# A selective-scan kernel: the convolved map is read piece by piece from DRAM, the decays move from PSUM to SBUF, and their banks become second buffers

## The chip, the cores and the metric

The kernel runs on one core of a Trainium2 chip. A core has five engines that run their own instruction streams and wait for each other by semaphores: PE (TensorE, matrix products), DVE (VectorE), ACT (ScalarE), POOL (GpSimd) and SP (SyncE, which here issues the transfers). SBUF is the working memory of 128 partitions; PSUM is the small memory of eight banks that PE writes its sums to. The metric is the device time in microseconds. The kernel before took 12172.9 us (median of three runs, 12171.95 to 12176.84).

## The reference, cut to what matters

Two layers of a state-space block run one after the other on 8 images of 64x64 positions and 96 channels. The first layer is the costly one. It projects 96 channels to 192, applies a 3x3 convolution per channel and a SiLU, which gives the map `xc`, and scans that map in four directions with 16 states per channel:

```python
xs = _cross_scan(xc)      # rows, columns, and both reversed
delta = softplus(dt_projs_w @ (x_proj_w @ xs)[:R] + bias)
def step(h, inp):
    u_t, d_t, B_t, C_t = inp
    dA = jnp.exp(d_t[..., None] * A)
    h = dA * h + d_t[..., None] * B_e * u_t[..., None]
    return (h, jnp.sum(h * C_e, axis=-1))
...
y = ys + u * D            # the skip term
y = _cross_merge(y)       # sum of the four directions
y = layernorm(y) * silu(z) @ out_proj_w.T
```

The second layer has a scan of the same kind whose sums matter only near the ends of the map, and the kernel computes only those (the "short" sets below).

## The kernel before

Positions lie along the free axis. The 192 channels are two halves (`h`) of 96 partitions. For the scan 32 channels x 4 states fill the 128 partitions, so one half is three groups (`g`) of 32 channels, and one group needs four sets (`i`) of four states. A set on 1024 positions is one recurrence on a 128x1024 tile. Per image there are four directions (`k`) x four pieces of 1024 positions ("units") x 2 halves x 3 groups x 4 sets = 384 sets, 3072 in all.

`scan_rows` writes the order of work out by hand: a loop over sets n, in which each engine gets what belongs to the sets around n. For a set, in this order:

- `fetch` (five sets ahead) has SP load `dt_rep` and `dtu_rep` (delta and delta*u of 32 channels, each copied to four partitions), once per group; `replicate` (four ahead) loads `b_rep` and `c_rep`.
- `fill` (one ahead, L940): ACT makes `decay` = exp(A x delta). The tile lies in PSUM, in the pool `pslot` of two buffers of two banks.
- `drive` (two ahead, L957): ACT copies delta*u of the group to PSUM, `pdrive`, one buffer of two banks.
- `advance_set` (L974 and L987): for three sets of four DVE multiplies `drive` by `b_rep` into `set`; for all four DVE then runs the scan in place, `set` = `decay` x previous + `set`. For the fourth set `early` has POOL make the product (L964), from SBUF's `dtu_rep`.
- `keep_state` (L998): ACT keeps the last column for the next piece.
- `read_out` (one behind, L1003): POOL multiplies `set` by `c_rep` into `out`.
- `collect` (three behind, L1030 and L1039): PE adds the old value of the sum (for the first direction the map times the skip weight `skip0`, for the others `y`) and gathers the states of each channel into `acc`, one PSUM bank; `release` (L1069) has ACT copy `acc` to `y`.

There are four `set` buffers and four `out` buffers. Between these, a plan of steps puts work of other stages into the same loop: `projection` and `ready_by_time` prepare a unit two units ahead (their PSUM bank is `pmisc`, one buffer), with POOL's delta*u (`take_product`, L606) and two stores by SP; `conv_beside` makes the second layer's map of the image before and the first layer's map of the image after, 512 positions at a time, with the bank of `pmisc`, and stores it to DRAM.

The map of an image, 32 KB per partition, lies whole in SBUF, in the pool `keep` of two buffers, the other being `y`. `next_map` loads the next image's map over the old one in four pieces near the end of the scan. PSUM is full: decays four banks, drive two, `acc` one, `pmisc` one.

The short sets of the second layer (48 in all, 960 columns) use the same buffers, with one more DVE multiplication (L977) by `cum_rep`.

Between two scans `between` runs the output phase (normalization, gate, output projection) of the image and prepares the first deltas of the next (`first_deltas`, `ready_first`, L658 to L660); `begin` does the first convolution and the first deltas; `finish` ends the last image.

Of the kernel before, what the change touches and what calls it, by code (L numbers as in the profile page):

```python
# [52 lines left out]
def two_ss2d_layers(ctx: ExitStack, tc: tile.TileContext, t: dict, out: bass.AP):  # L53
# [16 lines left out]
    keep = ctx.enter_context(tc.tile_pool(name="keep", bufs=2))  # L70
# [47 lines left out]
    w["skip0"] = const.tile([C, NH, C], F32, name="skip0")  # L118
    for h in range(NH):
        nc.vector.tensor_scalar(  # L120
            w["skip0"][:, h, :], w["eye"], w["dsum0"][:, h : h + 1], None, ALU.mult
        )

# [264 lines left out]

    def like(ap, by_column):

        return ap.rearrange("p (a b) -> p a b", b=HH) if by_column else ap
# [39 lines left out]
    def scan_rows(xc, y, parts, plan, rows, beside):  # L431

        with (
            tc.tile_pool(name="loads", bufs=2, side="right") as loads,
            tc.tile_pool(name="piece", bufs=1) as piece,
            tc.tile_pool(name="work", bufs=2) as work,
            tc.tile_pool(name="pslot", bufs=2, space=PSUM) as pslot,
            tc.tile_pool(name="pdrive", bufs=1, space=PSUM) as pdrive,
            tc.tile_pool(name="pacc", bufs=1, space=PSUM) as pacc,
            tc.tile_pool(name="pmisc", bufs=1, space=PSUM) as pmisc,
        ):  # L450
            units, jobs, sets, x_dbl = parts
            total = len(sets)
            plan = plan(pmisc)
            with tc.manual_schedule():
                state = None
                arena = piece.tile([P, 4 * T], F32, name="arena")
                plan.setdefault(-1, []).insert(0, lambda: low_rows(x_dbl, units[1], rows))
                for n in range(-AHEAD, max(total + 4, max(plan, default=0) + 1)):
                    at = lambda i: sets[n + i] if 0 <= n + i < total else None
                    m, j = divmod(n + 1, PER)  # L460
                    if j == 0 and 0 <= m < len(jobs):

                        stages = []
                        if m + 2 < len(jobs):
                            prepare = short_ready if jobs[m + 2]["unit"]["short"] else ready_by_time
                            stages += prepare(xc, x_dbl, jobs[m + 2], arena, pmisc)
                        if m % NH == 1 and m // NH + 2 < len(units):
                            unit = units[m // NH + 2]
                            project = short_projection if unit["short"] else projection
                            stages += project(xc, x_dbl, unit, rows, pmisc)  # L470
                        for step, stage in stages:
                            plan.setdefault(n + step, []).append(stage)
                    fetch(at(AHEAD), False, loads)
                    fetch(at(2), True, loads)
                    replicate(at(AHEAD_BC), x_dbl, loads)
                    replicate_short(at(AHEAD_BC), "b", loads)
                    replicate_short(at(AHEAD_BC - 1), "c", loads)
                    if at(0) and at(0)["unit"]["nth"] == 0 and at(0)["first"]:
                        state = piece.tile([P, D // GC * NS], F32, name="state0", bufs=2)
                    advance_set(at(0), state, work)  # L480
                    keep_state(at(-1))
                    fill(at(1), pslot)
                    drive(at(2), False, pdrive)
                    drive(at(1), True, pdrive)
                    release(at(-4), y, beside)
                    gate(at(1))
                    read_out(at(-1), work)
                    early(at(2), work)
                    late = (n + 1) % NS == 0
                    if not late:  # L490
                        collect(at(-3), xc, y, pacc)
                    for stage in plan.pop(n, []):
                        stage()
                    if late:
                        collect(at(-3), xc, y, pacc)
                assert not plan
# [70 lines left out]
    def projection(xc, x_dbl, unit, piece, pmisc):  # L567
# [4 lines left out]
        def product(s):  # L572
            at = slice(s * MM, (s + 1) * MM)
            unit["ps"] = pmisc.tile([P, MM], F32, tag="mm", name="ps_proj0")
            for hh in range(NH):
                nc.tensor.matmul(  # L576
                    unit["ps"][: 2 * ROWS, :],
                    w["wx0"][:, k % 2, hh, :],
                    positions(xc[:, hh, :], col, t0 + s * MM, MM),
                    start=hh == 0,  # L580
                    stop=hh == NH - 1,
                )
# [22 lines left out]
    def take_product(xc, job, col, t0):  # L605
# [3 lines left out]
            positions(xc[:, job["h"], :], col, t0, T),  # L609
# [8 lines left out]
    def ready_first(xc, x_dbl, job, piece, pmisc):  # L618
# [37 lines left out]
        def sums():  # L656
# [16 lines left out]
            (13, lambda: take_product(xc, job, col, t0)),  # L673
# [3 lines left out]
    def ready_by_time(xc, x_dbl, job, arena, pmisc):  # L677

        unit, h = job["unit"], job["h"]
        k, t0, col = unit["k"], unit["t0"], unit["column"]  # L680
# [61 lines left out]
        def product():  # L742
            job["dtu"] = arena[:C, HALF : HALF + T]
            take_product(xc, job, col, t0)
# [18 lines left out]
    def short_projection(xc, x_dbl, unit, piece, pmisc):  # L763
# [31 lines left out]
    def short_ready(xc, x_dbl, job, arena, pmisc):  # L795
# [209 lines left out]
    def collect(s, xc, y, pacc):  # L1005
# [21 lines left out]
        if s["i"] == 0:  # L1027
            old, lhs = (xc, w["skip0"][:, h, :]) if unit["k"] == 0 else (y, w["eye"])
            for acc, at in parts:
                nc.tensor.matmul(  # L1030
                    acc,
                    lhs[:, GC * g : GC * (g + 1)],
                    positions(old[:, h, :], unit["column"], unit["t0"] + at, n),
# [38 lines left out]
    def conv_beside(plan, pmisc, pool, edged, l, src, far, norm, starts, ends=None):  # L1072
# [50 lines left out]
        def store(job, c, h):  # L1123
            nc.sync.dma_start(far[:, h, c * MM : (c + 1) * MM], job["v"])
            if ends is None:
                return
# [57 lines left out]
    def next_map(b, i):  # L1184

        if i == 0:
            maps[b] = keep.tile([C, NH, L], F32, name="map")
        at = slice(i * T, (i + 1) * T)
        nc.sync.dma_start(maps[b][:, :, at], xc_far[b][:, :, at])

    def beside(b, pool):


        def make(pmisc):
# [12 lines left out]
            if b + 1 < NB:  # L1207
                xc_far[b + 1] = dram.tile([C, NH, L], F32, name="xc_far", bufs=2)
                conv_beside(
                    plan, pmisc, pool, edged, 0, t["x"][b + 1], xc_far[b + 1], norm0[b + 1],  # L1210
                    windows(16 if b >= 1 else 0, 16, b),
                )
                for i, step in enumerate((376, 378, 380, 388)):
                    plan.setdefault(step, []).append(lambda i=i: next_map(b + 1, i))
# [30 lines left out]
    def scan_last(b, xc):  # L1245
# [3 lines left out]
        with (  # L1249
# [10 lines left out]
            with tc.tile_pool(name="pmisc", bufs=4, space=PSUM) as pmisc:  # L1260
                for _, stage in short_projection(xc, None, unit, piece, pmisc):
                    stage()
                arena = piece.tile([P, 4 * T], F32, name="arena")
                for job in jobs:
                    for _, stage in short_ready(xc, None, job, arena, pmisc):
# [7 lines left out]
            with (  # L1273
# [5 lines left out]
                for n in range(-4, len(sets) + 4):  # L1279
# [9 lines left out]
                    collect(at(-2), xc, xc, pacc)  # L1289
# [387 lines left out]
    def first_deltas(b, xc, pool, bank):  # L1677

        units, jobs, sets, x_dbl = parts = scan_parts(b)
        stages = projection(xc, x_dbl, units[0], pool, bank)  # L1680
        for job in jobs[:NH]:
            stages += ready_first(xc, x_dbl, job, pool, bank)
        stages += projection(xc, x_dbl, units[1], pool, bank)
        return parts, [stage for _, stage in stages]

    def begin():

        with tc.tile_pool(name="pfirst", bufs=2, space=PSUM) as pfirst:
            bank = lambda name: pfirst.tile([P, MM], F32, tag="mm", name=name)
            xc = keep.tile([C, NH, L], F32, name="map")  # L1690
            with tc.tile_pool(name="first", bufs=1) as pool:
                norm0[0] = conv_first(t["x"][0], xc, pool, bank)
            with tc.tile_pool(name="before", bufs=1) as pool:
                parts, stages = first_deltas(0, xc, pool, pfirst)
                for stage in stages:
                    stage()
            if NB > 1:
                norm0[1] = first_norm(1, bank)
        return xc, parts
# [79 lines left out]
    def between(b, y):  # L1779

        st = stats_tile()
        xc = maps[b + 1]
        with (
# [11 lines left out]
            def beside(pmm):  # L1795
                bank = lambda name: pmm.tile([P, MM], F32, tag="mm", name=name)
                found["parts"], stages = first_deltas(b + 1, xc, before, pmm)
                steps = (1, 2, 2, 3) + (4, 5, 5, 6, 6, 7, 7, 6, 8, 9, 9)
# [27 lines left out]
        return xc, found["parts"]  # L1826

    def finish(b, y):
# [3 lines left out]
        with tc.tile_pool(name="x1T", bufs=1, side="right") as pool1:  # L1832
            x1T = pool1.tile([C, L], F32, name="x1T")
            with tc.tile_pool(name="last", bufs=1, side="right") as last:
                late_conv(1, last)
                xn = padded(last, "xn1")
                with tc.tile_pool(name="behind", bufs=1) as pool:
# [10 lines left out]
                    if b >= 1:  # L1848
                        streams.append(second_of(b - 1, keep, pool, pool, put))
# [19 lines left out]
    def general_second(b):  # L1869

        with tc.tile_pool(name="x1T", bufs=1) as pool1:
# [6 lines left out]
            xc, y = (keep.tile([C, NH, L], F32, name="map") for _ in range(2))  # L1878
# [21 lines left out]
    xc_far, xc1_far, ys_far, xs, maps, norm0, norm1 = ({} for _ in range(7))  # L1900
    xc, parts = begin()

    with tc.manual_schedule():
        for b in range(NB):
            y = keep.tile([C, NH, L], F32, name="map")
            with (
                tc.tile_pool(name="rows", bufs=1) as rows,
                tc.tile_pool(name="beside", bufs=1) as pool,
            ):
                scan_rows(xc, y, parts, beside(b, pool), rows, pool)  # L1910
            if b + 1 < NB:
                xc, parts = between(b, y)
# [101 lines left out]
```

## Time and profile before

| what | us |
|---|---|
| median of three runs | 12172.9 |
| the profiled execution's own time | 12189.3 |
| its span | 12187.5 |
| the eight scan stages together | 10356 |
| DVE busy in them | 9825 |
| POOL busy in them | 9634 |
| ACT busy in them | 7871 |
| PE busy in them | 7472 |

The span runs from the first to the last instruction. A scan stage is the stretch from the first scan of an image to its last; there are eight of some 1300 us each, with some 180 us between two of them, 201 us before the first and 416 us behind the last. The slices of the page show the eight stages as stretches of nines for DVE and POOL. In a group of instructions the columns are the line, the engine, the operation, the tiles, the shape and the count, then busy time and the mean of one instruction in ns, then the idle time of the engine just before them and what ended it. A line of a timeline gives start, length, engine, line and tiles; an instruction's length includes what it waits for after it has started.

### The profile page before, as it was taken

To read this page: it belongs to the slowest core of one execution; us is meant where nothing else is said; L and a number is where in the kernel's file an instruction comes from. 1 tells how busy PE (TensorE), PEld (TensorE's weight loads), DVE (VectorE), ACT (ScalarE), POOL (GpSimd) and SP (SyncE) were. 2 spreads that over 40 slices of the span, in tenths; PEclk is the share of its full clock that TensorE was granted. 3 is DMA by queue.
4 is the path that set the end of the run, shared out by engine and by line. 5 is a ranking of instruction groups with operands and counts; after the bars stand their busy time and mean duration, and the time that the engine had idled before them with its cause. 6 is when DMAs were issued, how large, how long until landed. Compare 5 with 4: busy or idle time off the path is not lost. (4 is left out here: it accounts for less than half of the span.)

```text
span 12187.5 us, 147673 instructions
## 1 busy us (share of the span) xinstructions
PE 8804.0 (72%) x50996; PEld 4018.9 (33%) x50996; DVE 10891.5 (89%) x6819; ACT 9067.0 (74%) x14930; POOL 10497.4 (86%) x4748
## 2 busy tenths in 40 slices
PE   5775577777777777776777777777687776876567
PEld 2332233332333323333233332333233332333222
DVE  6999889997999979999799997999979998899985
ACT  4777777777777777777778777787777777777775
POOL 3999889996999969999699986999879998799973
PEclk7776677778777887778877778777787777877667
DMA  3444444445444444444444444444544444444441
GB/s 96 166 153 156 138 161 155 160 163 153 153 161 164 164 142 165 153 160 160 144 167 163 164 151 155 163 155 160 174 131 165 164 164 156 146 150 158 159 142 59
DMA packets 670707, 1862.42 MB, mean 153 GB/s; under 512 B 186728, under 2 KB 201486, under 8 KB 669949
## 3 DMA queue, kind: packets, MB, share of 16 engines
q1 hardware_dynamic: 662781, 1840.30, 45.4%
q10 hardware_dynamic: 7168, 12.59, 0.3%
q8 instruction: 405, 6.64, 0.2%
q14 instruction: 353, 2.89, 0.1%
HBM read 1539.34 MB, written 313.28 MB: 152 GB/s over the span
## 5 line engine op out<-in xcount | busy, mean ns | idle before, releaser
L1003 POOL TENSOR_TENSOR out<-set,c_rep 128x1024 f32<-128x1024 f32 x3120 | 7305.7, 2361 | 826.4 <-PE acc L1039 329.8
L987 DVE TENSOR_TENSOR_SCAN set<-decay,state,set 128x1024 f32<-128x1024 f32 x2304 | 5360.5, 2344 | 350.5 <-ACT decay L940 112.6
L940 ACT ACTIVATE decay<-dt_rep,w_a 128x1024 f32<-128x1024 f32 x3072 | 3424.0, 1115 | 430.3 <-DVE set L987 428.9
L974 DVE TENSOR_TENSOR set<-drive,b_rep 128x1024 f32<-128x1024 f32 x2352 | 2819.2, 1199 | 26.3 <-ACT drive L957 16.0
L1039 PE MATMUL acc<-out,w_gather 128*32 128x256 f32 x24576 | 2384.5, 516 | 6.8 <-POOL out L1003 6.7
L1106 PE MATMUL ps_conv<-edged,taps 96*96 96x512 f32 (+1 forms) x4032 | 2198.5, 688 | 10.9 <-ACT arena L706 8.3
L964 POOL TENSOR_TENSOR set<-dtu_rep,b_rep 128x1024 f32<-128x1024 f32 x768 | 1853.7, 2414 | 89.5 <-DMA dt_far<-arena 39.1
L987 DVE TENSOR_TENSOR_SCAN set<-decay,set 128x1024 f32<-128x1024 f32 x768 | 1743.0, 2286 | 140.3 <-ACT decay L940 47.9
L728 PE MATMUL ps_sp<-w_eye,arena 128*96 128x128 f32 x7680 | 1162.0, 316 | 712.1 <-ACT arena L740 679.7
L1030 PE MATMUL acc<-map,w_eye 96*32 96x256 f32 x4608 | 577.1, 584 | 1359.0 <-ACT map L1069 1092.3
L1069 ACT COPY map<-acc 32x256 f32<-32x256 f32 x3072 | 1471.3, 479 | 66.2 <-PE acc L1039 25.8
L728 PEld LDWEIGHTS ps_sp<-w_eye,arena 128*96 128x96 f32 x7680 | 1005.7, 147 | 1017.6 <-ACT arena L740 795.1
L1039 PEld LDWEIGHTS acc<-out,w_gather 128*32 128x32 f32 x24576 | 878.3, 140 | 1382.9 <-issue 1072.0
L998 ACT COPY state<-set 128x1 f32<-128x1 f32 x2304 | 433.1, 188 | 1070.4 <-DVE set L987 1062.4
L694 PE MATMUL ps_dt<-w_dtw,x_dbl 7*128 7x96 f32 x3840 | 798.1, 370 | 498.7 <-ACT arena L740 423.1
L1106 PEld LDWEIGHTS ps_conv<-edged,taps 96*96 96x96 f32 (+1 forms) x4032 | 701.3, 189 | 1276.1 <-issue 1186.0
L694 PEld LDWEIGHTS ps_dt<-w_dtw,x_dbl 7*128 7x128 f32 x3840 | 695.3, 267 | 743.6 <-ACT arena L740 496.6
L957 ACT COPY drive<-dtu_rep 128x1024 f32<-128x1024 f32 (+1 forms) x816 | 816.5, 1001 | 33.5 <-DVE x_in L1651 13.5
L705 ACT ACTIVATE arena<-ps_dt 128x384 f32<-128x384 f32 x480 | 235.9, 492 | 620.8 <-PE ps_dt L694 597.4
L1030 PEld LDWEIGHTS acc<-map,w_eye 96*32 96x32 f32 x4608 | 104.1, 125 | 1679.8 <-ACT map L1069 1304.3
L606 POOL TENSOR_TENSOR arena<-arena,map 96x1024 f32<-96x1024 f32 x240 | 635.4, 2647 | 12.0 <-ACT arena L740 12.0
L576 PE MATMUL ps_proj<-map,w_wx 96*78 96x512 f32 x512 | 405.9, 931 | 13.7 <-ACT z L640 9.6
(202 smaller groups left out, 7682.4 us busy)
## 6 DMA issues: line engine op xcount, KB each, us to landing
dt_rep<-dt_far SPq DMA_DIRECT2D x768, 512.0 KB
dtu_rep<-dtu_far SPq DMA_DIRECT2D x768, 512.0 KB
b_rep<-x_dblr SPq DMA_DIRECT2D x256, 512.0 KB
c_rep<-x_dblr SPq DMA_DIRECT2D x256, 512.0 KB
b_rep<-x_dblc SPq DMA_DIRECT2D x256, 512.0 KB
c_rep<-x_dblc SPq DMA_DIRECT2D x256, 512.0 KB
dt_far<-arena SPq DMA_DIRECT2D x240, 384.0 KB
dtu_far<-arena SPq DMA_DIRECT2D x240, 384.0 KB
```

Of the source, the lines that this page charges most:

```text
L694: nc.tensor.matmul(job["ps"][:, j, :], unit["x_dbl"][: R + 1, at : at + P], w["dtw0"][:, k, h * C : (h + 1) * C], start=True, stop=True,)
L728: nc.tensor.matmul(job["ps"][:C, j * P : (j + 1) * P], job[name][:, s * BLOCKS + j, :], w["whole_eye"], is_transpose=True, start=i == 0, s ...
L940: nc.scalar.activation(s["decay"], s["group"]["dt"], AF.Exp, scale=rate)
L957: nc.scalar.copy(s["group"]["drive"], s["group"]["dtu"])
L964: nc.gpsimd.tensor_tensor(s["buf"], s["group"]["dtu"], b, ALU.mult)
L974: nc.vector.tensor_tensor(s["buf"], s["group"]["drive"], b, ALU.mult)
L987: nc.vector.tensor_tensor_scan(ordered(s["buf"], unit), ordered(s["decay"], unit), ordered(s["buf"], unit), 0.0 if unit["nth"] == 0 else s ...
L1003: nc.gpsimd.tensor_tensor(s["out"], s["buf"], s["unit"]["c", s["i"]], ALU.mult)
L1030: nc.tensor.matmul(acc, lhs[:, GC * g : GC * (g + 1)], positions(old[:, h, :], unit["column"], unit["t0"] + at, n), start=True, stop=False ...
L1039: nc.tensor.matmul(acc, w["gather"], s["out"][:, at : at + n], start=False, stop=s["i"] == NS - 1, skip_group_check=True,)
L1069: nc.scalar.copy(yk, like(acc, unit["column"]))
L1106: nc.tensor.matmul(job["ps"][:C, :], taps[l][:k, h, tap, :], edged[:k, tap // 3 : tap // 3 + rows, tap % 3 : tap % 3 + WW], start=tap == 0 ...
```

## The change

The map is no longer kept in SBUF. `store_maps` writes each piece of the map to DRAM twice, in row order and in column order (`xc_far` has two tensors), with four extra transfers per piece for the columns; `load_u` reads 1024 positions of both halves for a unit into `u` (two buffers of 8 KB per partition); `projection` and `take_product` read `u`. `next_map` is gone. The skip term is written by ACT (`skip_term`) into `y` before the first direction, so `collect` always starts from `y`, and `skip0` is gone. The pool `keep` has one buffer.

The space goes to the decays: `pslot` is now three buffers in SBUF. The four PSUM banks that they held become second buffers of `pdrive` (two more banks), `pacc` and `pmisc` (one each). `advance_set`, `fill` and `read_out` are as before, but the scan's `decay` lies in SBUF. On DVE and POOL the scan loop has the same instructions in the same order.

```diff
-    keep = ctx.enter_context(tc.tile_pool(name="keep", bufs=2))
+    keep = ctx.enter_context(tc.tile_pool(name="keep", bufs=1))
...
+    def store_maps(b, h, at, v):
+        far, far_col = xc_far[b]
+        nc.sync.dma_start(far[:, h, at], v)
+        rows = slice(at.start // WW, at.stop // WW)
+        for q in range(NT):
+            dst = far_col[:, h, q * T : (q + 1) * T].rearrange("p (a b) -> p a b", b=T // HH)
+            nc.sync.dma_start(dst[:, rows, :], by_piece(v)[:, q])
...
+    def load_u(b, unit):
+        t0 = unit["t0"]
+        unit["u"] = upool.tile([C, NH, T], F32, name="u")
+        src = xc_far[b][unit["column"]]
+        nc.sync.dma_start(unit["u"], src[:, :, t0 : t0 + T])
+
+    def skip_term(unit, h, y):
+        t0 = unit["t0"]
+        nc.scalar.mul(y[:, h, t0 : t0 + T], unit["u"][:, h, :], w["dsum0"][:, h : h + 1])
...
-            tc.tile_pool(name="pslot", bufs=2, space=PSUM) as pslot,
-            tc.tile_pool(name="pdrive", bufs=1, space=PSUM) as pdrive,
-            tc.tile_pool(name="pacc", bufs=1, space=PSUM) as pacc,
-            tc.tile_pool(name="pmisc", bufs=1, space=PSUM) as pmisc,
+            tc.tile_pool(name="slot", bufs=3) as pslot,
+            tc.tile_pool(name="pdrive", bufs=2, space=PSUM) as pdrive,
+            tc.tile_pool(name="pacc", bufs=2, space=PSUM) as pacc,
+            tc.tile_pool(name="pmisc", bufs=2, space=PSUM) as pmisc,
...
-                    positions(xc[:, hh, :], col, t0 + s * MM, MM),
+                    local(unit["u"][:, hh, :], col, s * MM, MM),
...
-            positions(xc[:, job["h"], :], col, t0, T),
+            local(job["unit"]["u"][:, job["h"], :], col, 0, T),
...
-            old, lhs = (xc, w["skip0"][:, h, :]) if unit["k"] == 0 else (y, w["eye"])
...
-                    lhs[:, GC * g : GC * (g + 1)],
-                    positions(old[:, h, :], unit["column"], unit["t0"] + at, n),
+                    w["eye"][:, GC * g : GC * (g + 1)],
+                    positions(y[:, h, :], unit["column"], unit["t0"] + at, n),
...
+            if ends is None:
+                store_maps(far, h, slice(c * MM, (c + 1) * MM), job["v"])
+                return
...
-                for i, step in enumerate((376, 378, 380, 388)):
-                    plan.setdefault(step, []).append(lambda i=i: next_map(b + 1, i))
```

In `begin` the first image's map is a tile of its own, whose pieces are stored to DRAM the same way and whose first two units are read from it by a transfer; in `between` the first two pieces are loaded at the first step.

## The prediction

> **What bounds the kernel now.** I read the engine totals first, then the groups by form, then a table of the eight scan stages, then two short timelines. The totals say that no engine is clearly behind:
>
> ```profile
> PE 8804.0 (72%) x50996; PEld 4018.9 (33%) x50996; DVE 10891.5 (89%) x6819; ACT 9067.0 (74%) x14930; POOL 10497.4 (86%) x4748
> ...
> q1 hardware_dynamic: 662781, 1840.30, 45.4%
> ```
>
> DVE and POOL are both close to full, and DMA is under half. The table of the eight scan stages (first scan to last scan of each image; columns: stretch, length, then busy time of each engine) is where the time is. In a row the busy times are those of PE, PEld, DVE, ACT and POOL; then come the granted clock, the DMA share and GB/s. One stage, and the sum of all eight:
>
> ```profile
> 1563.00:2868.00 1305.00, 972.19 (x5916) 454.48 (x5916) 1230.45 (x710) 993.37 (x1655) 1203.77 (x528) 0.77 0.47 160
> sum 10356.00, PE 7471.57 PEld 3538.07 DVE 9825.34 ACT 7871.03 POOL 9633.75; mean PE 933.95 PEld 442.26 DVE 1228.17 ACT 983.88 POOL 1204.22
> ```
>
> Of 12187.5 us of span 10355 us are scan, and there DVE is busy 95% and POOL 93%. So the stage lives on DVE and POOL running at the same time: 9825 + 9634 us of work are done in 10355. Everything depends on that overlap. The groups say what the two do (mean ns after the comma, then idle time before):
>
> ```profile
> L1003 POOL TENSOR_TENSOR out<-set,c_rep 128x1024 f32<-128x1024 f32 x3072 | 7199.4, 2363 | 633.9 <-PE acc L1039 329.8 <-DVE set L987 224.5 <-issue 29.4
> L987 DVE TENSOR_TENSOR_SCAN set<-decay,state,set 128x1024 f32<-128x1024 f32 x2304 | 5360.5, 2344 | 350.5 <-ACT decay L940 112.6 <-POOL set L964 62.4 <-DVE set L974 2.3
> L974 DVE TENSOR_TENSOR set<-drive,b_rep 128x1024 f32<-128x1024 f32 x2304 | 2764.5, 1200 | 17.9 <-DMA b_rep<-x_dblr 8.8 <-ACT drive L957 7.6 <-DMA out<-x_in 1.5
> L964 POOL TENSOR_TENSOR set<-dtu_rep,b_rep 128x1024 f32<-128x1024 f32 x768 | 1853.7, 2414 | 89.5 <-DMA dt_far<-arena 39.1 <-DMA b_rep<-x_dblr 24.0 <-DMA b_rep<-x_dblc 10.1
> L987 DVE TENSOR_TENSOR_SCAN set<-decay,set 128x1024 f32<-128x1024 f32 x768 | 1743.0, 2286 | 140.3 <-ACT decay L940 47.9 <-POOL set L964 35.2 <-ACT arena L709 1.1
> L606 POOL TENSOR_TENSOR arena<-arena,map 96x1024 f32<-96x1024 f32 x240 | 635.4, 2647 | 12.0 <-ACT arena L740 12.0
> ```
>
> Every DVE instruction in these rows has one of its two inputs in PSUM: the scan its decay, the product its drive. Elsewhere in the kernel a few have both inputs in SBUF, and they behave differently beside POOL. The view of line 659 (an addition of two SBUF tiles, minimum, median and maximum ns) and then the timelines of DVE and of POOL near 3000 us (start, length, both us):
>
> ```profile
> L659 DVE TENSOR_TENSOR ln<-ln,z x16: 1220/2174/3255, 150.4 to 10440.2; 96x1024 f32<-96x1024 f32 x16
> ```
>
> ```profile
> 3001.45 2.17 DVE L659 TENSOR_TENSOR ln<-ln,z 96x1024 f32<-96x1024 f32 x1
> 3003.66 3.25 DVE L660 TENSOR_TENSOR ln<-ln,dt 96x1024 f32<-96x1024 f32 x1
> 3006.84 1.21 DVE L1610 TENSOR_TENSOR y<-y,ps_mean 96x1024 f32<-96x1024 f32 x1
> ```
>
> ```profile
> 3000.51 2.04 POOL L1603 TENSOR_TENSOR sq<-sq 96x512 f32<-96x512 f32 x1 [0.96 <-ACT sq L1576]
> 3002.51 3.32 POOL L1606 TENSOR_TENSOR map<-map,sz 96x1024 f32<-96x1024 f32 x1
> ```
>
> POOL's L1603 ends at 3002.55 and L659 ends 1.07 after that; POOL's L1606 then ends 2.21 after L659 has ended (3003.62 to 3005.83), and L660 ends 1.08 after L1606. The two engines take turns, whole instructions at a time, although each had started before the other was done. L1610, with one input in PSUM, runs in 1.21 beside POOL. A second place shows it on full 128 partitions, during the short scans:
>
> ```profile
> 2889.02 2.26 DVE L977 SCALAR_TENSOR_TENSOR set<-cum_rep,set 128x960 f32<-128x960 f32 x1
> ```
>
> ```profile
> 2888.05 2.21 POOL L1003 TENSOR_TENSOR out<-set,c_rep 128x960 f32<-128x960 f32 x1 [3.42 <-DVE set L982]
> ```
>
> L977 (both inputs in SBUF, minimum 1.157 us) ends 1.02 after the POOL instruction ends. So **two SBUF inputs on DVE and a POOL instruction exclude each other**.
>
> **The change, part by part.**
>
> *Decays to SBUF.* The scan's inputs become decay and set, both SBUF. This is 3072 scans, every one of them beside POOL work. The lines above then turn the scan stage from two parallel streams into one serial one. A waiting instruction has its start-up behind it when its turn comes: L659 alone takes 1.22 and 1.08 within the alternation, so 0.14 is hidden; L1606 takes 2.20 after DVE's end where a POOL product of this size takes 2.36, so 0.16 is hidden. Turns then cost:
> - scans: 2304 x (2.344 - 0.139) + 768 x (2.286 - 0.139) = 6729 us;
> - read-outs: 3072 x (2.363 - 0.163) = 6758 us;
> - POOL's own products (L964): 768 x (2.414 - 0.16) = 1731 us;
> - delta*u (L606): 240 x (2.647 - 0.16) = 597 us.
>
> Sum 15815 us for the eight stages, against 10355 now: **+5460 us**. DVE's 2304 products (1.20 each, one input PSUM) lie beside POOL's turns and cost nothing; their cover is the 2.2 us turn of POOL. Behind a waiting scan DVE's next drive product and the next map's products (L1119) queue, and ACT's state copy and decay wait for it; behind a waiting read-out POOL's own products and delta*u queue, and PE's gather and SP's delta stores wait. Each has a stage half as long again to catch up. Someone always wants the turn: POOL has five instructions to DVE's four scans per group, and four set buffers let DVE run ahead. Lower end: all scans at 2.147 and all POOL instructions at 2.20 give 6596 + 8976 = 15572, +5217. Upper end: nothing hidden, durations end to end, 5401 + 1756 + 7259 + 1854 + 635 = 16905, +6550. I take the first, because the timelines show the hidden part directly.
>
> [...]
>
> *Scan time itself.* A product of 1024 columns with both inputs in SBUF takes 1.220 alone (least of L659), and 1.200 with one in PSUM (L974): no gain from leaving PSUM, at most 0.02 x 3072 = 61 us either way. [...]
>
> *Third decay buffer, second buffers for drive, acc and misc.* What they can remove is DVE's idle time in the stage, at most 10355 - 9825 = 530 us. Once the turns bind, none of it is on the path: 0. ACT writes decays to SBUF instead of PSUM; it has 984 of 1294 us per stage now and would have nearly 2000, so a tenth more per exponential would hide too.
>
> *Skip term.* PE's first matmuls read y rather than the map; ACT gains 64 scalings of 96x1024, about 1.14 each by the like scaling at L1725: 73 us over eight stages, hidden under ACT's slack. If ACT were full they would cost 73.
>
> *Map pieces.* 128 loads of 768 KB replace 28 map loads of the same size, and stores of the next map gain four DMAs each: 112 x 4, plus 8 x 5 at the start, so with the 100 loads 588 more issues on SP at the 0.3 to 0.45 us of its issues, some 220 us of a queue that mostly waits. The column copies are cut into runs of 16 floats: 112 x 4 x 768 + 8 x 4 x 1536 = 393216. By the queue row a packet costs 0.454 x 16 x 12187.5 / 662781 = 0.134 us at most for so small a run, so 0 to 3.3 ms of each DMA engine: with today's 5.5 that is at most half of 17.7 ms. Hidden; in a 12 ms kernel it would be 72%. At the start 49152 of these lie ahead of the first deltas' stores on SP's queue: 0 to 410 us, I take 30, since the convolution before it leaves the queues idle. In each of the seven stages between scans the first projection waits on PE's queue for a piece instead of finding the map in place: 0 to 6 us each, I take 3, 20 in all; the normalization's matmuls queue behind it.
>
> *Short scans* (48 sets): scans and read-outs already follow each other (L1003 idle 3.42 until the scan ends), so 0.
>
> **Sum.** The profiled execution took 12189.3 (span 12187.5), 16 above the median of the runs. 12189 + 5460 + 50 = 17699; less 16, **17,680 us**.
>
> **Rivals.**
> 1. *The scan does not exclude POOL.* For it: no scan in this trace has two SBUF inputs, and it is twice as slow per column as a product, so it reads half as often. Against: L977 and L659. Then only the idle time is at stake: 12189 - 530 + 50 = 11,710 at best, 12,240 at worst. It decides if fewer than 530 / 5460, a tenth, of the scans have to take turns.
> 2. *Turns by reads, not by instruction.* The scan blocks POOL only for the 1.08 it would need at full rate: 3072 x 1.08 + 9086 = 12404, +2049, so about 14,290. Against: both waits above end with the other's last column.
> 3. *Turns are lost.* If neither is ready 5% of the time, as DVE in the stage now, 790 more: 18,470; with no start-up hidden and a slow start 19,100.
>
> **Chances.** Turns by whole instruction, losses included: 0.88; rival 2: 0.06; rival 1: 0.06, of which 0.01 within 0.2% (24 us, about what a measurement of this kernel tells from no change). The first case reaches from 12189 + 5217 = 17,400 to about 19,000. The range 17,250 to 18,800 takes in the lower end with a little for scans that hold less, and rival 3's middle, and leaves out the other rivals and the far end: about 0.8. Faster 0.05, same 0.01, slower 0.94.
>
> **What would show it.** Scan rows at a mean of 3.3 to 3.9 us instead of 2.3, read-outs at 3.8 to 4.4 instead of 2.36, the drive product still at 1.20, scan stages of about 1980 us, DVE and POOL both near full while ACT and PE fall to around 50%. A scan that keeps 2.3 us beside POOL makes the prediction wrong, as does a stage where DVE idles on DMA.

## The result and the profile after

The changed kernel takes **17,701.9 us** (median, 17,699.6 to 17,711.0) against 12,172.4 for the kernel before in the same comparison: a ratio of 1.4545, 95% interval 1.4519 to 1.4570. The forecast was 17,680. The profiled execution has a span of 17,700.9 us.

The totals of the changed kernel, and the line of its main DMA queue:

```profile
PE 10686.8 (60%) x50996; PEld 4388.1 (25%) x50996; DVE 15501.1 (88%) x6817; ACT 9238.8 (52%) x14994; POOL 15646.5 (88%) x4748
...
q1 hardware_dynamic: 1085373, 1947.30, 35.4%
```

DVE and POOL have 4610 and 5149 us more "busy" time, with the same instructions in the scan loop. The table of the eight scan stages, one stage and the sum:

```profile
6626.00:8604.00 1978.00, 1231.98 (x5940) 507.33 (x5940) 1794.50 (x710) 1020.61 (x1671) 1851.66 (x531) 0.66 0.35 110
...
sum 15838.00, PE 9348.77 PEld 3901.98 DVE 14400.04 ACT 8082.69 POOL 14753.52; mean PE 1168.60 PEld 487.75 DVE 1800.01 ACT 1010.34 POOL 1844.19
```

From first to last scan the eight stages take 15,841 us instead of 10,355: +5486 of the +5513 of the span. All that lies around them grew by 27 us. The groups by form (the same code as before, 39 lines further down: the read-out of L1003 is now L1042, and L1003 is POOL's own product) show who got longer:

```profile
L1042 POOL TENSOR_TENSOR out<-set,c_rep 128x1024 f32<-128x1024 f32 x3072 | 10724.9, 3512 | 1099.9 <-DVE set L1026 963.3 <-issue 113.0 <-DVE lowest_short L923 6.9
L1026 DVE TENSOR_TENSOR_SCAN set<-decay,state,set 128x1024 f32<-128x1024 f32 x2304 | 8680.2, 3776 | 1087.7 <-POOL set L1003 896.5 <-ACT decay L979 7.8 <-ACT map L1107 7.2
L979 ACT ACTIVATE decay<-dt_rep,w_a 128x1024 f32<-128x1024 f32 x3072 | 3518.2, 1146 | 1418.5 <-DVE set L1026 1416.2 <-ACT state L1037 0.6
...
L1003 POOL TENSOR_TENSOR set<-dtu_rep,b_rep 128x1024 f32<-128x1024 f32 x768 | 2979.3, 3879 | 8.4 <-DMA edged<-x 8.4
L1026 DVE TENSOR_TENSOR_SCAN set<-decay,set 128x1024 f32<-128x1024 f32 x768 | 2920.4, 3812 | 351.7 <-POOL set L1003 274.0 <-ACT decay L979 16.8 <-ACT map L1107 2.2
L1013 DVE TENSOR_TENSOR set<-drive,b_rep 128x1024 f32<-128x1024 f32 x2304 | 2752.3, 1195 | 19.4 <-DMA b_rep<-x_dblr 6.8 <-ACT drive L996 6.5 <-DMA out<-x_in 6.1
```

The scan went from 2.34 to 3.78 us, POOL's read-out from 2.36 to 3.51, POOL's product from 2.41 to 3.88. DVE's product, whose drive stayed in PSUM, kept its 1.20. The view of the scan's line (minimum, median, maximum in ns), and then a stretch of the two engines' timelines:

```profile
L1026 DVE TENSOR_TENSOR_SCAN set<-decay,state,set x2304: 2318/3134/10631, 312.2 to 17282.8; 128x1024 f32<-128x1024 f32 x192
```

```profile
3004.56 3.10 DVE L1026 TENSOR_TENSOR_SCAN set<-decay,state,set 128x1024 f32<-128x1024 f32 x1
3009.90 6.78 DVE L1026 TENSOR_TENSOR_SCAN set<-decay,state,set 128x1024 f32<-128x1024 f32 x1 [2.24 <-POOL set L1003]
3016.60 1.19 DVE L1013 TENSOR_TENSOR set<-drive,b_rep 128x1024 f32<-128x1024 f32 x1
```

```profile
3005.48 4.39 POOL L1003 TENSOR_TENSOR set<-dtu_rep,b_rep 128x1024 f32<-128x1024 f32 x1
3009.83 4.69 POOL L1042 TENSOR_TENSOR out<-set,c_rep 128x1024 f32<-128x1024 f32 x2
3016.82 2.36 POOL L1042 TENSOR_TENSOR out<-set,c_rep 128x1024 f32<-128x1024 f32 x1 [2.30 <-DVE set L1026]
```

The first scan ends at 3007.66, and POOL's L1003, which had started at 3005.48, ends 2.21 later. The second scan starts at 3009.90, 0.07 after the first of two read-outs; the second read-out ends at 3014.52, and the scan 2.16 after it. The second read-out went ahead of a scan that had been waiting since before the first one ended. A scan that has to wait ends 2.15 us after the last POOL instruction that it waited for, however long it had waited: that is the median over the 2986 scans of this trace during which a POOL instruction ends (the end of the scan minus the end of that instruction); for 98% of them it lies between 2.145 and 2.155.

### The profile page after: what moved, and what is told of

It is laid out like the page before. It is cut to its first block, busy times and chain, and to the rows that moved or that the text cites. A ratio compares the mean times of both kernels' runs of the same rounds, so it can differ in the third digit from the quotient of the medians.

```text
span 17700.9 us, 147646 instructions
## 1 busy us (share of the span) xinstructions
PE 10686.8 (60%) x50996; PEld 4388.1 (25%) x50996; DVE 15501.1 (88%) x6817; ACT 9238.8 (52%) x14994; POOL 15646.5 (88%) x4748
## 3 DMA queue, kind: packets, MB, share of 16 engines
q1 hardware_dynamic: 1085373, 1947.30, 35.4%
## 5 line engine op out<-in xcount | busy, mean ns | idle before, releaser
L1042 POOL TENSOR_TENSOR out<-set,c_rep 128x1024 f32<-128x1024 f32 x3120 | 10831.2, 3492 | 1264.0 <-DVE set L1026 963.3
L1026 DVE TENSOR_TENSOR_SCAN set<-decay,state,set 128x1024 f32<-128x1024 f32 x2304 | 8680.2, 3776 | 1087.7 <-POOL set L1003 896.5
L1077 PE MATMUL acc<-out,w_gather 128*32 128x256 f32 x24576 | 3174.3, 558 | 3575.2 <-POOL out L1042 3569.9
L1026 DVE TENSOR_TENSOR_SCAN set<-decay,set 128x1024 f32<-128x1024 f32 x768 | 2920.4, 3812 | 351.7 <-POOL set L1003 274.0
L1003 POOL TENSOR_TENSOR set<-dtu_rep,b_rep 128x1024 f32<-128x1024 f32 x768 | 2979.3, 3879 | 8.4 <-DMA edged<-x 8.4
L1144 PE MATMUL ps_conv<-edged,taps 96*96 96x512 f32 (+1 forms) x4032 | 2950.0, 890 | 21.0 <-issue 8.2
L1068 PE MATMUL acc<-map,w_eye 96*32 96x256 f32 x6144 | 1485.0, 584 | 2257.6 <-ACT map L1107 2255.5
L1068 PEld LDWEIGHTS acc<-map,w_eye 96*32 96x32 f32 x6144 | 400.4, 131 | 3208.5 <-ACT map L1107 2971.3
L645 POOL TENSOR_TENSOR arena<-arena,u 96x1024 f32<-96x1024 f32 x240 | 1107.0, 4613 | 0.0
L614 PE MATMUL ps_proj<-u,w_wx 96*78 96x512 f32 x512 | 420.9, 963 | 82.4 <-DMA u<-xc_farr 44.3
```

Of the source, the lines that this page charges most:

```text
L645: nc.gpsimd.tensor_tensor(like(job["dtu"], col), like(job["dt"], col), local(job["unit"]["u"][:, job["h"], :], col, 0, T), ALU.mult,)
L1003: nc.gpsimd.tensor_tensor(s["buf"], s["group"]["dtu"], b, ALU.mult)
L1026: nc.vector.tensor_tensor_scan(ordered(s["buf"], unit), ordered(s["decay"], unit), ordered(s["buf"], unit), 0.0 if unit["nth"] == 0 else s ...
L1042: nc.gpsimd.tensor_tensor(s["out"], s["buf"], s["unit"]["c", s["i"]], ALU.mult)
L1068: nc.tensor.matmul(acc, w["eye"][:, GC * g : GC * (g + 1)], positions(y[:, h, :], unit["column"], unit["t0"] + at, n), start=True, stop=False,
L1077: nc.tensor.matmul(acc, w["gather"], s["out"][:, at : at + n], start=False, stop=s["i"] == NS - 1, skip_group_check=True,)
```

## The experiments

Figures for stages are from the first to the last scan of each image, summed over eight. Runs with one measurement have no interval; their differences here are far larger than the spread of the others.

**Undo the decays, keep the pieces.** The decays go back to two PSUM buffers, drive, acc and misc to one buffer each.

```diff
-            tc.tile_pool(name="slot", bufs=3) as pslot,
-            tc.tile_pool(name="pdrive", bufs=2, space=PSUM) as pdrive,
-            tc.tile_pool(name="pacc", bufs=2, space=PSUM) as pacc,
-            tc.tile_pool(name="pmisc", bufs=2, space=PSUM) as pmisc,
+            tc.tile_pool(name="pslot", bufs=2, space=PSUM) as pslot,
+            tc.tile_pool(name="pdrive", bufs=1, space=PSUM) as pdrive,
+            tc.tile_pool(name="pacc", bufs=1, space=PSUM) as pacc,
+            tc.tile_pool(name="pmisc", bufs=1, space=PSUM) as pmisc,
```

> The changed kernel with the decays back in two PSUM buffers and one buffer each for drive, acc and misc; the map is still read piece by piece. Turn theory: nothing of the added 5530 us is left, scan rows back at 2.29 and 2.34 us, read-outs at 2.36; 12,150 to 12,300 us, the upper part if the pieces, the skip term on ACT and the column runs cost something. Rival (the small column runs and the loads crowd the transfers, part of the loss is theirs): over 12,500.

Measured: 12,386.1 us, ratio to before 1.0181 (1.0164 to 1.0198). Stages 10,499, so of the 5486 us in the stages 5342 are undone with the decays. But 215 us remain, which puts the time above the expectation's upper end and below the rival's. They are taken up again below.

**Keep the decays in SBUF, undo only the second banks.**

```diff
-            tc.tile_pool(name="pdrive", bufs=2, space=PSUM) as pdrive,
-            tc.tile_pool(name="pacc", bufs=2, space=PSUM) as pacc,
-            tc.tile_pool(name="pmisc", bufs=2, space=PSUM) as pmisc,
+            tc.tile_pool(name="pdrive", bufs=1, space=PSUM) as pdrive,
+            tc.tile_pool(name="pacc", bufs=1, space=PSUM) as pacc,
+            tc.tile_pool(name="pmisc", bufs=1, space=PSUM) as pmisc,
```

> The changed kernel with one buffer each for drive, acc and misc again (their second banks unused), decays in three SBUF buffers. Prediction's reading (the turns bind and what the banks free is not on the path): 17,660 to 17,760 us. Rival (the second banks take waits out of the longer stage, so that the turns alone would have cost more): 17,900 us or more.

Measured: 17,702.1 us (17,697.5 to 17,711.8), the same as the changed kernel. The banks move waits of PE (for POOL's read-out 3570 us in the changed kernel and 1071 here, for ACT's copies 2256 and 3619), but no time. The run answers another question too. The granted TensorE clock fell with the change, from 0.77 to 0.66 in the stages shown; here it is lower still (0.640 over the execution against 0.674) in the same time, so the clock is not what costs.

**The same decays, another second input.** All decays stay in SBUF; for three sets of four DVE writes its product to PSUM, so that these scans have one input in each memory.

```diff
+            tc.tile_pool(name="pprod", bufs=2, space=PSUM) as pprod,
...
+                s["prod"] = pprod.tile([P, T], F32, name="prod")
...
-            nc.vector.tensor_tensor(s["buf"], s["group"]["drive"], b, ALU.mult)
+            nc.vector.tensor_tensor(s["prod"], s["group"]["drive"], b, ALU.mult)
...
-            ordered(s["buf"], unit),
+            ordered(s["prod"], unit),
             0.0 if unit["nth"] == 0 else s["last"],
```

> The changed kernel with all decays in SBUF, but for three sets of four DVE writes its product to two PSUM buffers, so that these scans read one input from SBUF (the decay) and one from PSUM; drive, acc and misc have one buffer each. The fourth scan still has two SBUF inputs. Theory of two SBUF inputs: as with every fourth decay in SBUF, 13,400 to 13,900 us, scans of the three sets at 2.3 us. Rival (a decay in SBUF is slow by itself): 17,000 us or more, all scans beyond 3.3 us.

Measured: 13,622.6 us, as the theory of two SBUF inputs has it. The groups of scans (state means that the piece goes on from the one before):

```profile
L1033 DVE TENSOR_TENSOR_SCAN set<-decay,state,prod 128x1024 f32<-128x1024 f32 x1728 | 4055.7, 2347 | 253.4 <-ACT decay L980 41.1 <-DVE prod L1018 2.4 <-POOL set L1004 1.0
...
L1033 DVE TENSOR_TENSOR_SCAN set<-decay,state,set 128x1024 f32<-128x1024 f32 x576 | 2192.6, 3807 | 214.2 <-POOL set L1004 161.6 <-ACT decay L980 50.0 <-ACT state L1044 1.5
L1033 DVE TENSOR_TENSOR_SCAN set<-decay,prod 128x1024 f32<-128x1024 f32 x576 | 1317.1, 2287 | 91.5 <-ACT decay L980 22.4 <-POOL set L1004 0.5 <-POOL arena L646 0.5
L1033 DVE TENSOR_TENSOR_SCAN set<-decay,set 128x1024 f32<-128x1024 f32 x192 | 807.3, 4205 | 78.2 <-POOL set L1004 63.0 <-ACT decay L980 12.3 <-ACT arena L749 2.9
```

Within one kernel, beside the same POOL work, a scan of an SBUF decay and a PSUM product takes 2.35 us, and a scan of two SBUF tiles 3.81. So a decay in SBUF is not slow by itself; in the kernel before, a set in SBUF with its decay in PSUM took 2.34. Only both inputs in SBUF together cost.

**How the cost grows with the number of scans.** Only every fourth decay in SBUF.

```diff
-                    fill(at(1), pslot)
+                    fill(at(1), slot if at(1) and by_gpsimd(at(1)) else pslot)
```

> As the kernel with pieces only, but the decay of every fourth set (768 of 3072 scans) lies in SBUF. Turn theory: per group of four sets POOL has its own 12.1 us and one scan's turn of 2.15, DVE its own 12.9 and a wait of about 1: 14.0 to 14.7 us per group against 13.5, so 12,600 to 13,100 us. A cost in proportion (a fixed price per scan with two SBUF inputs, a quarter of 5460): 13,500. If the place of the decay does not matter: 12,200.

Measured: 13,648.2 us. My own band fell; the price in proportion was near. The stages take 11,761, that is 1262 more than with the pieces alone, or 1.64 us for each of 768 scans; with all 3072 it is 5342 / 3072 = 1.74. The three scans of four whose decay is in PSUM keep a mean of 2.33. The fourth has 3.96, which is 1.67 above its 2.29 before, where I had counted a wait of about 1. The view of the scans says why:

```profile
L1027 DVE TENSOR_TENSOR_SCAN set<-decay,state,set x2304: 2324/2350/6819, 278.1 to 13226.0; 128x1024 f32<-128x1024 f32 x192
```

A scan can take 6.82, which is its turn of 2.15 and two POOL instructions of 2.34: it waits not for one but for two. Of the 768 scans 291 wait through two POOL instructions, 404 through one.

**Another DVE instruction with two SBUF inputs.** Decays in PSUM, the drive in SBUF.

```diff
-            tc.tile_pool(name="slot", bufs=3) as pslot,
-            tc.tile_pool(name="pdrive", bufs=2, space=PSUM) as pdrive,
+            tc.tile_pool(name="pslot", bufs=2, space=PSUM) as pslot,
+            tc.tile_pool(name="drive", bufs=2) as pdrive,
```

> The changed kernel with the decays back in PSUM and the drive in two SBUF buffers instead (acc and misc keep their second banks). Now the scan has one SBUF input and 2304 products of DVE have two. Turn theory: the turns add up to 2304 x 1.07 + 9090 = 11,550 us for the stages, and DVE's own work with an average wait of 1.1 before each product to about 12,400; 13,400 to 14,400 us in all, products at 1.8 to 2.5 us instead of 1.20, scans at 2.3. Rival (something in the scan alone takes turns): 12,200, products at 1.2.

Measured: 14,842.7 us, above the band, and far from the rival. The two DVE groups have changed places:

```profile
L1013 DVE TENSOR_TENSOR set<-drive,b_rep 128x1024 f32<-128x1024 f32 x2352 | 5575.2, 2370 | 27.4 <-ACT drive L996 13.6
L1026 DVE TENSOR_TENSOR_SCAN set<-decay,state,set 128x1024 f32<-128x1024 f32 x2304 | 5352.2, 2344 | 240.4 <-ACT decay L979 58.1
```

Now the product waits (2.37) and the scan does not (2.34). The band was missed for the same reason as before, as the view of the product's line shows (minimum, median, maximum):

```profile
L1013 DVE TENSOR_TENSOR set<-drive,b_rep x2352: 1130/1423/8467, 159.9 to 14749.4; 128x1024 f32<-128x1024 f32 x192, 128x960 f32<-128x960 f32 x4
```

Of the 2304 long products 1578 wait, and 257 of these through two or three POOL instructions. They end 1.08 after the last of them (median), the turn that the forecast had read from L659 and L660.

**Must POOL read?** Each read-out is replaced by two fills.

```diff
-            nc.gpsimd.tensor_tensor(s["out"], s["buf"], s["unit"]["c", s["i"]], ALU.mult)
+            for _ in range(2):
+                nc.gpsimd.memset(s["out"], 0.0)
```

> The changed kernel with every read-out on POOL replaced by two fills of the out tile with zero, which write SBUF and read nothing; the multiplication by C is left out. POOL's own products and delta*u are kept. Theory that only a POOL instruction that reads SBUF takes turns with the scan: DVE's own 9.9 ms for the stages and 1.0 to 2.2 us for each of 1008 reading instructions, 12,300 to 13,800 us; scans at 2.4 to 2.9 us. Rival (any POOL instruction takes turns): turns of 2.15 us for the scan and some 0.9 for each fill, 14.4 ms of turns in the stages, 15,500 to 16,500 us, scans beyond 3.2 us.

Measured: 12,911.4 us. The groups of POOL, and DVE's larger group of scans:

```profile
L1043 POOL MEMSET out<- 128x1024 f32 x6144 | 5755.3, 953 | 1643.2 <-PE acc L1078 1466.1
L1003 POOL TENSOR_TENSOR set<-dtu_rep,b_rep 128x1024 f32<-128x1024 f32 x768 | 2176.4, 2834 | 101.1 <-DVE set L1026 29.5 <-issue 17.4 <-ACT state L1037 16.7
```

```profile
L1026 DVE TENSOR_TENSOR_SCAN set<-decay,state,set 128x1024 f32<-128x1024 f32 x2304 | 6102.5, 2669 | 190.5 <-ACT decay L979 8.4 <-POOL set L1003 4.4 <-DVE set L1013 0.9
```

The fills write 128x1024 in 0.95 us beside scans of two SBUF inputs, and the scan's mean stays at 2.67, with the 1008 instructions that read left to wait for. The trace separates the two. 2073 scans have no end of a reading POOL instruction within them, and take 2.33 beside the fills. The other 999 have one, and end 2.15 after it. So the POOL instructions that read SBUF take turns with the scan, and the fills do not.

**Where the pieces' 215 us come from.** First the column copies in long runs, with the same number of transfers and bytes.

```diff
-            dst = far_col[:, h, q * T : (q + 1) * T].rearrange("p (a b) -> p a b", b=T // HH)
-            nc.sync.dma_start(dst[:, rows, :], by_piece(v)[:, q])
+            n = (at.stop - at.start) // NT
+            start = q * T + rows.start * (T // HH)
+            nc.sync.dma_start(far_col[:, h, start : start + n], v[:, q * n : (q + 1) * n])
```

> The kernel with pieces only, with the column copies of the map written in runs of 128 floats (256 at the start) instead of 16; the reordering to columns is left out, the number of transfers and their bytes are the same. If the 215 us that the pieces cost come from the 393216 small packets: 12,180 to 12,270 us and DMA share near 46%. If they come from the number of issues on SP or from the loads: 12,350 to 12,400 us.

Measured: 12,276.7 us, ratio 1.0094 (1.0077 to 1.0110): half of the 215 us went with the small packets, half stayed, so neither reading alone holds. The queue's share was 49.2% with pieces alone and 47.9% here. The stages tell the two halves apart. From the kernel before to the one with pieces alone they grew by 145 us (10,355 to 10,499), and the stretches around them by 52 (1833 to 1885). With the long runs the stages are down to 10,384, and the stretches stay at 1885: there PE waits 47 us for the first pieces of the images.

Then more room for the copies of B and C:

```diff
-AHEAD_BC = 4
+AHEAD_BC = 7
...
-                rep = loads.tile([P, T], F32, tag="bc_rep", name=f"{c}_rep", bufs=2 * NS + 1)
+                rep = loads.tile([P, T], F32, tag="bc_rep", name=f"{c}_rep", bufs=2 * NS + 4)
```

> The kernel with pieces only, with the SBUF that the map left free given to the copies of B and C: 12 instead of 9 buffers, loaded seven sets ahead instead of four. If the pieces' 215 us are waits for late copies of B (POOL's own product idles 241 us instead of 90, DVE then waits 211 us for it instead of 98): 12,170 to 12,280 us, perhaps below the kernel before. If the lateness is elsewhere: 12,350 to 12,400 us.

Measured: 12,169.2 us, ratio to before 1.0002 (0.9992 to 1.0012): all 215 us are back, with all the small packets still there. POOL's product, and DVE's waits for it (us, times, longest), with pieces alone and then here:

```profile
L1003 POOL TENSOR_TENSOR set<-dtu_rep,b_rep 128x1024 f32<-128x1024 f32 x768 | 1857.6, 2419 | 241.5 <-issue 78.5
...
DVE set L1026 <- POOL set L1003: 210.6, 126, 5.5
```

```profile
L1003 POOL TENSOR_TENSOR set<-dtu_rep,b_rep 128x1024 f32<-128x1024 f32 x768 | 1843.0, 2400 | 0.0
...
DVE set L1026 <- POOL set L1003: 51.9, 90, 1.9
```

The idle time before it is gone, and DVE's waits for it fell from 211 to 52 us. So in the stages the pieces delayed the copies of B, and POOL's product, and with it the fourth scan. The stages are now at 10,284 us, 71 below those of the kernel before, so the room does more than undo their delay of 145; the stretches around them stay at 1881. Whether the room would help the kernel before as well was not tried, since its SBUF holds the map there. Whether the 29 us that long runs leave in the stages come from the issues or from the loads, these runs do not separate. More buffers elsewhere did not help:

```diff
-SETS = 4
+SETS = 6
...
-            s["out"] = work.tile([P, T], F32, name="out", bufs=4)[:, : s["unit"]["n"]]
+            s["out"] = work.tile([P, T], F32, name="out", bufs=5)[:, : s["unit"]["n"]]
```

> As the kernel with pieces only, with the SBUF that the map left free given to six set buffers and five out buffers instead of four and four. If DVE's 98 us of waits for POOL's own product, and POOL's 330 us for a free out buffer, come from the buffer counts: 50 to 200 us faster than pieces only, below the kernel before. If DVE's waits for decays take their place: the same as pieces only within 0.3%.

Measured: 12,426.4 us, ratio 1.0221 (1.0204 to 1.0238): no gain but 40 us more than with pieces alone, 0.3%, at the edge of the second reading. POOL no longer waits for an out buffer, but for DVE (472 us instead of 228), and its own product for the copies of B (242 us).

**A version faster than both.** In the kernel with 12 copies, PE still waits seven times, 45 us in all, for the first piece of an image:

```profile
PE ps_proj L614 <- DMA u<-xc_farr: 45.3, 7, 7.7
```

The first two loads of an image move to the end of the scan before.

```diff
+                ahead_parts[b + 1] = scan_parts(b + 1)
+                for step, unit in zip((376, 378), ahead_parts[b + 1][0]):
+                    plan.setdefault(step, []).append(lambda u=unit: load_u(b + 1, u))
```

> The kernel with pieces and 12 copies of B and C, with the first two pieces of the next image loaded at steps 376 and 378 of the scan instead of at the first step of the output phase. There PE waits seven times, 45 us in all, for a piece, and the stretches between scans are 48 us longer than in the kernel before. If those are the same: 12,110 to 12,140 us, 0.2 to 0.5% below the kernel before. If another wait takes their place (the copies of B and C, the normalization's own): 12,160 to 12,180 us.

Measured: 12,113.2 us, ratio to before 0.9960 (0.9946 to 0.9974). PE no longer waits for a piece. The stretches around the scans fell from 1881 to 1819 us (1833 before), the stages are at 10,268; the profiled execution is the fastest of the five, 24 us below their median.

Then a fifth out buffer on top:

```diff
-            s["out"] = work.tile([P, T], F32, name="out", bufs=4)[:, : s["unit"]["n"]]
+            s["out"] = work.tile([P, T], F32, name="out", bufs=5)[:, : s["unit"]["n"]]
```

> As the kernel with the early pieces, with five out buffers instead of four. POOL idles 330 us for a free out buffer (PE's gather behind ACT's copies). If that idle time is what makes POOL's own product late for DVE (52 us of waits): 20 to 50 us less than with early pieces alone. If DVE and ACT set the pace: no difference beyond 0.2%.

Measured: 12,110.5 us, ratio 0.9952 (0.9938 to 0.9966), the same as without the fifth buffer within 0.2%: the second reading. Its stretches around the scans are at 1838, its stages at 10,267.

## Why the prediction was right

*The turns.* The step that decided, two SBUF inputs on DVE against a POOL instruction, held for the scan, which the trace before did not contain in that form. Its sum was 15,815 us for the stages; they took 15,841. The measured terms come from the trace: the ends of all scans, read-outs, products and delta*u instructions are put in order, and each instruction gets the time from the end before its own to its own end. So the terms add up to the stages:

| term | forecast us | measured us |
|---|---|---|
| 3072 scans | 6729 | 6625 (median 2.149 each) |
| 3072 read-outs | 6758 | 6903 (3056 of them; 16 end behind the last scan of a stage) |
| 768 products on POOL | 1731 | 1731 |
| 240 delta*u | 597 | 582 |

Two sizes were off and nearly cancelled, so it is in part luck that 17,680 comes within 0.2% of 17,702. The scan that continues from a state needs no more of a turn than one that does not (2.149 both; I had kept their difference of 0.058), and 0.195 of its 2.344 is hidden where I had taken 0.139 from an addition. And the read-out cost 2.16 only behind a scan while already waiting (1784 of them); 877 came right behind another POOL instruction at 2.32, and 411 started only once the scan had ended, at 2.59.

*Alternation.* "Someone always wants the turn" nearly held; that a waiting scan comes next after one POOL instruction did not. Of the 2986 that wait, 439 do so through more than one, and some through four (10.63 us). The sum does not care, since a turn is used by either. The signs named for the profile do: read-outs have a mean of 3.51, below the 3.8 to 4.4 forecast, and DVE is busy 91% of the stages, POOL 93%, rather than full, since POOL running ahead leaves DVE to wait for POOL's product (1171 us). The scan's 3.78 lies within its 3.3 to 3.9, the product stayed at 1.20, the stages are 1980, ACT and PE at 52 and 60%.

*Third decay buffer and second banks* at nothing: shown for the banks by the kernel with single banks. No run took the third decay buffer away alone; DVE idles 25 us for decays in the changed kernel.

*Scan time itself:* a scan that does not wait takes as long with both inputs in SBUF as with its decay in PSUM. Its least time is 2.318 us in the view of L1026 above and 2.321 in the kernel before:

```profile
L987 DVE TENSOR_TENSOR_SCAN set<-decay,state,set x2304: 2321/2349/2354, 279.0 to 11769.1; 128x1024 f32<-128x1024 f32 x192
```

The prediction's sentence that two SBUF inputs on DVE and a POOL instruction exclude each other was too wide: a scan of two SBUF inputs that waits ends 2.149 us after a POOL instruction that reads SBUF, but one beside the fills alone, which only write it, takes 2.33. That cost nothing here, since POOL's long instructions in the stages all read SBUF.

*Pieces.* Hidden in this kernel, as forecast: +27 us around the stages where I had 50. The first scan starts at 195 instead of 201 us, so the 30 for the start were not there; in the seven output phases PE waited 44 us for a piece where I had 20. The DMA share in a 12 ms kernel, up to 72% by the bound, is 49%. But the bound on DMA share did not see the real price without the turns: 215 us, most of it by late copies of B in the stages, the rest around them, with the queue at 49%.

*Rivals.* The scan that does not exclude POOL (11,710 to 12,240) and turns by reads (14,290) are out: scans take 3.78 us beside POOL, and one that waits ends a full 2.15 after POOL, not 1.08. Lost turns, the third rival, are a small part of its 790 us: the 411 read-outs that started late cost 0.39 each beyond the 2.20 forecast, 160 us in all.

## What to carry to other kernels

Before moving an operand from PSUM to SBUF, count the SBUF inputs of each DVE instruction that reads it, and look in the trace for any DVE instruction with two SBUF inputs beside POOL: its minimum and maximum, and the ends of the two engines, show in a few lines whether the streams run beside each other or in turn. If they take turns, add the turns up: here the forecast sum of 15,815 us stood against 15,841 measured, and second PSUM buffers did nothing for it (17,701.9 us with them, 17,702.1 without). And look where a late load releases an instruction on another engine: the added transfers cost 215 us here, most of it by late copies of B before POOL's product, and more room for those copies paid it back.

## What the runs showed that I had not expected

A DVE instruction that waits for POOL is not always served after the POOL instruction in progress: scans of 6.8 us in the kernel with every fourth decay in SBUF, up to 10.6 in the changed kernel, products up to 8.5 with the drive in SBUF. It goes with this that a mixed load costs nearly as much per scan (1.64 us for a quarter of them) as the full one (1.74).

The small packets took little of the queue's time themselves: 347,136 more (1,085,373 against 738,237 on the queue, small runs against long ones, same bytes) raised the time that the packets took from 5877 us (0.479 of 12,268.5) to 6093 us (0.492 of 12,383.7) on each of 16 engines: an estimate of 0.01 us for each small packet. It is rough, since the other runs with the same packets lie between 6088 us (0.490 of 12,423.8) and 6266 (0.354 of 17,700.9).
